# Quarter-width third blocks in the experts, a rotation on TensorE and other moved work at both ends of attention

## The chip, the cores and the metric

The kernel runs on one NeuronCore of a Trainium2 chip. Its engines work in parallel, each on its own stream of instructions in program order: PE (TensorE, matrix products, with PEld for the loads of its weights), DVE (VectorE), ACT (ScalarE), POOL (GpSimd) and SP (SyncE, which here only issues DMAs). The metric is the device time of one execution in microseconds (us). Before the change it was 4768.45 us, the median of 3 runs (4766.24 to 4772.63). A separate execution was profiled; every duration below comes from that one. Line numbers such as L761 are those of the kernel before.

## What is computed

The reference is one layer of the macaron kind: half an expert layer, attention, half an expert layer, each on a layer norm and each added to its input (8 sequences of 1024 rows, 512 wide, float32):

```
x = x + 0.5 * ffn(_layernorm(x))
x = x + attn(_layernorm(x))
x = x + 0.5 * ffn(_layernorm(x))

def ffn(x):                       # 32 experts, C = ceil(1.25 * 8192 / 32) = 320
    top1 = argmax(softmax(xt @ w_router));  gate = its probability
    pos = rank of the token among those of its expert;  accepted = pos < C
    y = (silu(buf @ w_gate) * (buf @ w_up)) @ w_down       # per expert, 320 rows
    return xt + where(accepted, y[slot] * gate, 0)

def attn(x):                      # 16 heads of 32
    q, k, v = x @ Wq.T + bq, x @ Wk.T + bk, x @ Wv.T + bv
    q, k = rope(q), rope(k)       # x * cos + rotate_half(x) * sin
    return softmax(q @ k.T / sqrt(32)) @ v @ Wo.T + bo
```

## The kernel before

**Stages.** First all rows are normalized and routed (`front`): a table in DRAM gets, for each slot of each expert, the token's number and its gate. Then the experts of the first half layer run one after the other (`experts`), then attention (`Attention.run`), whose last part also routes its result, then the experts of the second half layer. PE, DVE, ACT and POOL execute in exactly the order in which the program issues (a manual schedule); SP's DMAs are ordered by a scheduler.

**Experts.** They are sorted by their number of tokens, most first, and the code exists in four versions with fixed widths by rank (`profiles`); a switch takes the narrowest that holds all tokens. Version 0 has widths 320 (6 experts), 304 (1), 288 (5), 272 (6), 256 (3), 240 (5), 224 (3), 208 (3). An expert's rows lie in up to three blocks of 128 rows; the third holds at most 64 tokens (`last`). `feed` (L722) computes one expert: for each of four quarters f of the hidden width, `gated` (L706) makes 4 products for the gate and 4 for the up half (L712, moving size the width), ACT makes the Silu and DVE the product `a` (L736). In the same time DVE and ACT measure and normalize the rows of the following expert. Then for each block the product with `w_down` follows: 4 products of 512 columns for a full block (L753); for the third block each token takes two partitions: its 64 tokens go through two halves of the array's columns, once for the first 256 output columns and once for the last 256 (L761, 8 products of 256 columns). DVE adds the gated product to the rest of the rows (L757; L767 for the third block, 256 columns) and POOL issues the indirect DMA that puts the rows back (L771). `places` (L566) reads the table once per half layer and makes `come` (which rows to gather), `go` (where to put) and `gates`, with the third block's entries doubled for the two halves. Float32 products run as two passes, so the profile counts twice as many.

**Attention** runs over 8 sequences b and 4 groups c of four heads. `opening` (L1072) is what runs before the first products of scores: SP loads two weights and then 8 tiles of x; DVE measures a tile (`measure`), POOL takes the power -0.5, ACT normalizes, PE transposes four blocks (`turn`) and DVE (half 0) or ACT (half 1) copies the result to `hT` (`kept`, L1147). Tiles of half 0 are transposed while those of half 1 are measured. Then `project` makes k and q of half 0 (4 products each), and `rotated` (L1207) applies the rotation: DVE adds the bias and writes `raw` (L1215), 8 DMAs issued by SP exchange the halves of each head into `rot` (L1222, L1223), POOL multiplies `raw` by the cosines (L1225), DVE multiplies `rot` by the sines and adds (L1228, L1229). Only then do the scores start.

`stage` (L894) has 16 slots. A slot computes the scores `sa` (L1295) of one pair of stretches for all four heads, from which DVE takes maxima (L1310) and ACT the exponentials (L1314, `junk`), and from the second stage on also the transposed scores `sb` of the unit before, whose exponentials `pr` (L1307) are multiplied by v into `po` (L1377, `weighed`). Between, a slot has one group of products from `fill`: projections of q and k, of v (`values`), or of the output (`output`, L1387). All of these accumulate in one bank of PSUM with the tag `m`. Scores use three places `s0`, `s1`, `s2`. The first stage (b = c = 0) has no `sb` and `po`; its first 13 slots each hold a whole group.

**Attention's end.** A last stage finishes the sums of the last unit and fills slots 9 to 12 with the output of half 0 of the last sequence; in slot 14 the task `finished(b, 0)` starts, which normalizes and routes those 4 tiles: ACT normalizes (`last_rows`, L1469) and writes the kept part `rs` (`put_kept`), PE transposes, ACT copies (L214), PE computes the router's products (`routers`, L231 and L243), DVE and PE the positions (`route`), POOL scatters into the table. Behind the stage the outputs of half 1 follow, four groups, each with two steps of the task between; then `finished(b, 1)` with `sorted`, which ranks the experts for the switch. Then SP reads the table and the second experts start.

Of the kernel before, what the change touches and what calls it, by code (L numbers as in the profile page):

```python
# [22 lines left out]
P = 128  # L23
# [27 lines left out]
class Block:  # L51


    def __init__(self, nc, tc, T, D, E, F):
# [20 lines left out]
        assert all(a <= b for one, two in zip(self.profiles, self.profiles[1:])  # L75
                   for a, b in zip(one, two))

        self.copy = nc.scalar.copy
# [123 lines left out]
    def logits(self, hs, lg, pool, psum, tag, bufs=2, tags=None):  # L202

        xT = pool.tile([P, self.KD, 4 * P], F32, tag="xT", bufs=bufs, name="xT")
        j = 0
        for h in hs:
            if isinstance(h, tuple):
                yield h  # L210
                continue
            yield PE, 0.6
            if tags:
                self.nc.scalar.copy(  # L214
                    xT[:, :, j * P : (j + 1) * P], self.turned(psum, tags[j], h)
                )
            else:
                self.transposed(psum, tag, xT[:, :, j * P : (j + 1) * P], h)
            j += 1
        yield from self.routers(xT, lg, pool, psum, tag, bufs=1)  # L220
# [289 lines left out]
    def experts(self, table, ranks, src, dst, weights, loaded=None, others=None):  # L510
# [16 lines left out]
        for i in tc.Switch(which, len(self.profiles)):  # L527
            widths = self.profiles[i]
            with (
# [12 lines left out]
                following = expert.gather(1, widths[1])  # L542
                for r in range(E):
                    if following:
                        following.weights = self.load(
                            wp, order, r + 1, weights, hold=None if r else "wg"
                        )
# [6 lines left out]
class Expert:  # L554
# [7 lines left out]
    def places(self, table, matrix):  # L562
# [9 lines left out]
        )  # L572
        rows = ap.tile([R, P, 2], F32, tag="slots", bufs=1, name="slots")
        nc.sync.dma_start(rows, table[0 : s.NS, :].rearrange("(r s) c -> r s c", s=P))
# [8 lines left out]
        for i in range(2):  # L583
            p = slice(i * n, (i + 1) * n)
            nc.vector.tensor_scalar(
                self.go[p, R - E : R], ids[p, R - E : R], 2.0, float(i), ALU.mult, ALU.add
            )

    def begin(self, to):
# [87 lines left out]
    def rests(self, to):  # L677

        s, n, half = self.s, self.s.last, self.s.D // 2
        for i in range(min(to.NB, s.NB - 1)):  # L680
            s.rest(to.x[:, i, :], to.x[:, i, :], to.by, i)
        if to.NB == s.NB:
            to.rest = self.ap.tile([P, half], F32, tag="rest", name="rest")
            for i in range(2):
                p = slice(i * n, (i + 1) * n)
                s.rest(
                    to.rest[p, :], to.x[p, s.NB - 1, i * half : (i + 1) * half], to.by,
                    s.NB - 1, p,
                )
# [30 lines left out]
    def feed(self, now, following, after):  # L720
# [3 lines left out]
        nc, s = self.nc, self.s  # L724
        n, half, KF = s.last, s.D // 2, s.KF
        a, wd = s.acts[now.r % 2], now.weights[2]
# [14 lines left out]
        for i in range(now.NB):  # L741
# [16 lines left out]
            else:  # L758
                for f in range(KF):
                    for c in range(2):  # L760
                        nc.tensor.matmul(  # L761
                            yp[c * n : (c + 1) * n, 0:half], a[:, f, i * P : s.C],
                            wd[:, f, c * half : (c + 1) * half],
                            start=(f == 0), stop=(f == KF - 1),
                        )
                ys = ys[:, 0:half]
                nc.vector.scalar_tensor_tensor(  # L767
                    ys, yp[:, 0:half], gate, now.rest, ALU.mult, ALU.add
                )
                to = to.rearrange("t (c d) -> (t c) d", c=2)  # L770
            nc.gpsimd.indirect_dma_start(  # L771
# [6 lines left out]
class Attention:  # L778
# [13 lines left out]
    def __init__(  # L792
# [14 lines left out]
        self.tasks, self.behind, self.half, self.now = [], [], None, 0  # L807
        self.credit, self.biased = 0.0, False
        self.hT, self.w_qk, self.qk, self.v, self.oT = ({} for _ in range(5))
# [113 lines left out]
    def run(self):  # L923
        nc, tc = self.nc, self.tc
        F, KD = mybir.EngineType, self.KD
        with (
# [6 lines left out]
            with tc.manual_schedule(engines={F.PE, F.Activation, F.DVE, F.Pool}):  # L933
                self.s.copy = nc.vector.tensor_copy
                later = self.opening()
                units = [(b, c) for b in range(self.B) for c in range(KD)]
                for i, (b, c) in enumerate(units):
                    self.stage(
                        (b, c), units[i - 1] if i else None, self.fill(b, c, later),
# [4 lines left out]
                    None, units[-1], dict(zip((9, 10, 11, 12), self.output(b, 0))),  # L944
                    {14: [(2, self.finished(b, 0))]}, whole=True,
                )
                self.last_sums()
                for f in self.output(b, 1):
                    at_once(f())
                    self.now += 1  # L950
                    for _ in range(2):
                        self.step(100)
                        self.product()
                self.start(self.finished(b, 1, self.ranked))
# [54 lines left out]
    def constants(self, wp):  # L1009
# [5 lines left out]
        for i, a in enumerate((bq, bk, bv)):  # L1015
# [4 lines left out]
            self.bias[:, 0, :], self.bias[:, 0, :], self.scale, None, ALU.mult  # L1020
        )
        self.ident16 = wp.tile([P, P], BF16, name="ident16")
        nc.vector.tensor_copy(self.ident16, s.ident)
# [76 lines left out]
    def opening(self):  # L1100
# [40 lines left out]

        def turn(half, j):
            x = xs[half][j]
            s.normalize(x, x, bys[half][1], j)
            return s.turned(psum, f"s{j % 3}", x)

        def kept(half, j, tp):  # L1147
            copy = nc.scalar.copy if half else nc.vector.tensor_copy
            copy(self.hT[0, half][:, :, j * P : (j + 1) * P], tp)  # L1149

        for j in range(4):
            measure(0, j)
        for j in range(4):
            measure(1, j)
            kept(0, j, turn(0, j))
        at_once(steps[-1])
        self.there |= {(0, 0), (0, 1)}
        q0, k0, k1, q1 = self.project(0, 0)
        for f in (k0, q0):
            at_once(f())  # L1160
        for j in range(4):
            kept(1, j, turn(1, j))
            self.now += 1
            self.step(100)
        self.load(2)
        while self.tasks:
            self.now += 1
            self.step(100)
        return [k1, q1]
# [9 lines left out]

    def project(self, b, c):  # L1180

# [7 lines left out]
        for which, n in ((0, 0), (1, 0), (1, 1), (0, 1)):  # L1189

            def group(n=n, which=which):
                assert (b, n) in self.there, (b, c, n)
                if n == 0:
                    name = "qk"[which]
                    dst[which] = pool.tile([P, self.L], F32, tag=name, bufs=3, name=name)
                acc = self.psum.tile([P, 512], F32, tag="m", name="pq")
                for k in range(KD):
# [5 lines left out]
                    )  # L1203
                self.start(self.rotated(dst[which], b, c, which, n, acc), rank=0)

            work.append(group)
        return work  # L1207

    def rotated(self, dst, b, c, which, n, acc):
# [22 lines left out]
    def values(self, b):  # L1232
# [3 lines left out]
        for t in range(LT):  # L1236

            def group(t=t):
                v = self.pool.tile([P, D], F32, tag="v", bufs=12, name="v")
                acc = self.psum.tile([P, D], F32, tag="m", name="pv")  # L1240
                hT, at = self.hT[b, t // 4], t % 4 * P
# [188 lines left out]
    def finished(self, b, half, counted=None):  # L1430
# [39 lines left out]
        def last_rows():  # L1470
            while self.weighted < half:
                yield WAIT, 1
            for j, x in enumerate(self.kept[half]):
                h = pool.tile([P, D], F32, tag="h3", bufs=3, name="h3")
                s.normalize(h, x, by, j)
                if not half:
                    put_kept(j)
                yield h

# [129 lines left out]
```

## Time and profile before

| stage of the profiled execution | us from the start | length | PE busy | DVE busy | ACT busy | granted PE clock |
|---|---|---|---|---|---|---|
| normalizing and routing | 0 to 176 | 176.0 | 102.6 | 129.9 | 92.4 | 0.74 |
| first experts | 176 to 930 | 754.0 | 753.9 | 275.5 | 153.1 | 1.00 |
| attention's opening | 930 to 972.3 | 42.3 | 16.7 | 18.2 | 9.8 | 0.67 |
| its first stage | 972.3 to 1051 | 78.7 | 70.1 | 58.3 | 48.3 | 0.96 |
| stages between and sums of the last | 1051 to 3911 | 2860.0 | 2803.0 | 2025.8 | 2510.8 | 1.00 |
| last outputs, routing, first gather | 3911 to 3990 | 79.0 | 37.4 | 26.6 | 19.4 | 0.65 |
| second experts | 3990 to 4756 | 766.0 | 755.2 | 276.7 | 108.8 | 0.99 |

The profiled execution took 4757.85 us, of which its span, from the first to the last record, is 4756.0 us. The table is a view by windows: for each stretch the time in which each engine was busy, and the mean clock that PE was granted as a share of full speed. A busy PE need not be at its peak, since products overlap in the array.

### The profile page before, as it was taken

To read this page: it belongs to the slowest core of one execution; us is meant where nothing else is said; L and a number is where in the kernel's file an instruction comes from. 1 tells how busy PE (TensorE), PEld (TensorE's weight loads), DVE (VectorE), ACT (ScalarE), POOL (GpSimd) and SP (SyncE) were. 2 spreads that over 40 slices of the span, in tenths; PEclk is the share of its full clock that TensorE was granted. 3 is DMA by queue.
4 is the path that set the end of the run, shared out by engine and by line. 5 is a ranking of instruction groups with operands and counts; after the bars stand their busy time and mean duration, and the time that the engine had idled before them with its cause. 6 is when DMAs were issued, how large, how long until landed. Compare 5 with 4: busy or idle time off the path is not lost.

```text
span 4756.0 us, 68742 instructions
## 1 busy us (share of the span) xinstructions
PE 4538.9 (95%) x24532; PEld 2114.6 (44%) x24532; DVE 2811.0 (59%) x5542; ACT 2942.7 (62%) x5890; POOL 788.9 (17%) x798
## 2 busy tenths in 40 slices
PE   6799999888999999999999999999999986999999
PEld 4466677632233333333333333333333324666777
DVE  8433333367667777767767767777777743333332
ACT  6211212159998888888888888888888861111111
POOL 4433333210000000100010110110110002222221
PEclk7899999989999999999999999999999997999999
DMA  4556666511112212212212212212212114555564
GB/s 144 164 178 205 196 201 231 198 30 37 35 30 61 75 39 65 72 39 68 71 39 67 70 43 65 72 39 70 67 41 58 52 41 150 168 173 175 177 207 141
DMA packets 288503, 482.09 MB, mean 101 GB/s; under 512 B 47608, under 2 KB 82882, under 8 KB 288146
## 3 DMA queue, kind: packets, MB, share of 16 engines
q1 hardware_dynamic: 253554, 400.95, 26.9%
q0 software_dynamic: 34304, 76.41, 5.2%
q8 instruction: 196, 3.21, 0.3%
q14 instruction: 161, 1.32, 0.1%
q10 hardware_dynamic: 288, 0.20, 0.0%
HBM read 376.18 MB, written 89.46 MB: 98 GB/s over the span
## 4 chain that ended last, share of the span: by engine, by line
PE 82%; DVE 7%; ACT 4%; issue 3%; DMA 2%; POOL 1%; SPq 1%; DVEq 0%; POOLq 0%; ACTq 0%
PE sa L1295 13%; PE gp L712 9%; PE up L712 9%; PE pq L1200 9%; PE po L1377 9%; PE yp L753 9%; PE sb L1275 6%; PE px L1411 4%; PE pv L1245 4%; PE sb L1302 3%; ACT junk L1314 2%; DVE nm L1310 2%; PE yp L761 1%; PE tp L700 1%; PE tp L196 1%
## 5 line engine op out<-in xcount | busy, mean ns | idle before, releaser
L1310 DVE TENSOR_REDUCE nm<-sa 128x2 f32<-128x1024 f32 x1024 | 1249.0, 1221 | 652.0 <-PE sa L1295 392.3
L1314 ACT ACTIVATE junk<-sa,nm 128x512 f32<-128x512 f32 x2048 | 1407.3, 687 | 271.9 <-DVE nm L1310 191.7
L1295 PE MATMUL sa<-k,q 32*128 32x512 f32 x4096 | 1144.6, 643 | 13.0 <-ACT pr L1307 4.2
L1307 ACT ACTIVATE pr<-sb 128x1024 f32<-128x1024 f32 x1024 | 1040.7, 1018 | 107.8 <-PE sb L1302 104.4
L1302 PE MATMUL sb<-q,k 32*128 32x512 f32 x4096 | 1063.4, 603 | 0.0
L717 ACT ACTIVATE sg<-gp 128x320 f32<-128x320 f32 (+7 forms) x256 | 99.6, 389 | 1122.1 <-PE gp L712 1120.9
L1225 POOL TENSOR_TENSOR raw<-raw,a 128x512 f32<-128x512 f32 x128 | 164.5, 1285 | 2388.7 <-DMA rot<-raw 1571.3
L1377 PE MATMUL po<-pr,v 128*32 128x512 f32 x4096 | 549.4, 608 | 0.1
L1200 PE MATMUL pq<-hT,wqk 128*128 128x512 f32 x1024 | 507.6, 619 | 8.0 <-DVE hT L1149 4.4
L712 PE MATMUL gp<-bT,wg 128*128 128x272 f32 (+7 forms) x2048 | 509.2, 392 | 0.0
L712 PE MATMUL up<-bT,wu 128*128 128x272 f32 (+7 forms) x2048 | 503.5, 389 | 0.0
L753 PE MATMUL yp<-wd,a 128*128 128x512 f32 x1024 | 460.3, 592 | 0.0
L1275 PE MATMUL sb<-mrow,ones 3*128 3x512 bf16 x2048 | 393.0, 385 | 43.7 <-ACT pr L1307 41.2
L712 PEld LDWEIGHTS gp<-bT,wg 128*128 128x128 f32 x2048 | 384.7, 191 | 98.4 <-issue 26.7
L712 PEld LDWEIGHTS up<-bT,wu 128*128 128x128 f32 x2048 | 386.6, 190 | 75.4
L1275 PEld LDWEIGHTS <-ones 3*128 3x128 bf16 x2048 | 99.6, 91 | 712.8 <-issue 673.2
L736 DVE TENSOR_TENSOR a<-sg,up 128x320 f32<-128x320 f32 (+7 forms) x256 | 110.7, 433 | 506.5 <-PE up L712 368.9
L1314 ACT ACTIVATION_READ_ACCUMULATOR junk<-sa,nm 128x1 f32 x2048 | 398.1, 194 | 0.0
L1302 PEld LDWEIGHTS sb<-q,k 32*128 32x128 f32 x4096 | 360.3, 184 | 0.1
L1295 PEld LDWEIGHTS sa<-k,q 32*128 32x128 f32 x4096 | 303.2, 183 | 70.7 <-ACT pr L1307 30.4
L1200 PEld LDWEIGHTS pq<-hT,wqk 128*128 128x128 f32 x1024 | 175.0, 190 | 324.5 <-issue 225.3
L757 DVE SCALAR_TENSOR_TENSOR ys<-yp,gates,x 128x512 f32<-128x512 f32 x128 | 96.1, 751 | 337.2 <-PE yp L753 337.2
(183 smaller groups left out, 4231.5 us busy)
## 6 DMA issues: line engine op xcount, KB each, us to landing
wg<-in_w_gate SPq DMA_DIRECT2D x64, 1024.0 KB
wu<-in_w_up SPq DMA_DIRECT2D x64, 1024.0 KB
wd<-in_w_down SPq DMA_DIRECT2D x64, 1024.0 KB
rot<-raw SPq DMA_DIRECT2D x1024, 32.0 KB
all<-in_x SPq DMA_DIRECT2D x32, 512.0 KB
xt<-first_rows SPq DMA_DIRECT2D x64, 256.0 KB
xr<-first_rows SPq DMA_DIRECT2D x64, 256.0 KB
d<-inverse SPq DMA_DIRECT2D x256, 64.0 KB
```

What stands on the lines that cost most here:

```text
L712: nc.tensor.matmul(acc, w[:, k, f * P : (f + 1) * P], to.bT[:, k, 0:width], start=(k == 0), stop=(k == s.KD - 1),)
L753: nc.tensor.matmul(yp, a[:, f, i * P : (i + 1) * P], wd[:, f, :], start=(f == 0), stop=(f == KF - 1),)
L1200: nc.tensor.matmul(acc, w[:, which, k, :], self.hT[b, n][:, k, :], start=(k == 0), stop=(k == KD - 1),)
L1245: nc.tensor.matmul(acc, hT[:, k, at : at + P], self.w_vo[:, k, :], start=(k == 0), stop=(k == KD - 1),)
L1275: nc.tensor.matmul(sb[:, h, :], self.ones16[at : at + 3, :], row[at : at + 3, :], start=True, stop=False,)
L1295: nc.tensor.matmul(sa[:, h, :], qa[at, (g * 4 + j) * P : (g * 4 + j + 1) * P], ka[at, m * 512 : (m + 1) * 512], start=True, stop=True,)
L1302: nc.tensor.matmul(sb[:, h, :], k[at, t * P : (t + 1) * P], q[at, n * 512 : (n + 1) * 512], start=False, stop=True,)
L1307: nc.scalar.activation(pr, sb, AF.Exp)
L1310: nc.vector.tensor_reduce(nm[:, m, j, pair : pair + 2], sa, AX.X, ALU.max, negate=True)
L1314: nc.scalar.activation(self.junk, sa[:, h - pair, :], AF.Exp, bias=nm[:, m, j, h : h + 1], accum_out=se[:, m, j, h : h + 1],)
L1377: nc.tensor.matmul(self.po[at : at + HD, :], self.v[b][t][:, c * P + at : c * P + at + HD], prs[h // 2 * 2][:, h % 2, :], start=(t == 0), ...
L1411: nc.tensor.matmul(acc, self.oT[b, c, half][:, j * P : (j + 1) * P], self.w_vo[:, c, :], start=False, stop=(c == KD - 1),)
```

## The change

1. **Third blocks of at most 32 tokens by quarters.** For widths over 256 and up to 288 a token takes four partitions, each with 128 output columns: 16 products of 32 weight columns and 128 moving columns in place of 8 of 64 and 256. `rest`, the DVE sum and the scattered rows follow. A new function makes the table entries for these experts, once per half layer, before expert 2 is fed.
2. **Opening.** Half 0 is measured, transposed and copied (ACT and DVE in turn) ahead of the measuring of half 1; k and q of half 0 are projected into two banks; their bias is added on ACT, and the exchange of halves is a product with a permutation (`turn`, built by 8 small POOL copies) instead of 8 DMAs each.
3. **First stage.** Its groups accumulate in the banks `m` and `po` in turn.
4. **Ends.** `finished(b, 0)` starts in slot 13 instead of 14; one step instead of two between the last output groups; copies of the router's transposes alternate between ACT and DVE; the last four rows are all normalized first, two on ACT and two on DVE.

```diff
+    def parts(self, width):
+        s = self.s
+        return 1 if width <= (s.NB - 1) * P else 4 if width <= s.quarter else 2
+    def quarters(self, widths):
+        few = [r for r, width in enumerate(widths) if self.parts(width) == 4]
...
+        nc.vector.tensor_copy(
+            rows[last, :, :],
+            self.rows[last, 0:n, :].rearrange("r s c -> r (s c)").unsqueeze(1)
+            .to_broadcast([E, 4, n * 2]),
+        )
+        for i in range(2):
+            pt = self.ps.tile([P, len(few)], F32, tag="tp", name="pt")
+            nc.tensor.matmul(
+                pt, rows[last, :, i], self.matrix[last, at], start=True, stop=True
+            )
+            if i == 0:
+                nc.vector.tensor_scalar(self.come[:, at], pt, float(s.T - 1), None, ALU.min)
+                for k in range(4):
...
+                    nc.vector.tensor_scalar(
+                        self.go[p, at], pt[p, :], 4.0, float(k), ALU.mult, ALU.add
+                    )
+            else:
+                nc.vector.tensor_copy(self.gates[:, at], pt)
@@ experts
                 for r in range(E):
+                    if r == 2:
+                        expert.quarters(widths)
@@ feed
-                    for c in range(2):
+                    for c in range(parts):
                         nc.tensor.matmul(
-                            yp[c * n : (c + 1) * n, 0:half], a[:, f, i * P : s.C],
-                            wd[:, f, c * half : (c + 1) * half],
+                            yp[c * n : (c + 1) * n, 0:part], a[:, f, i * P : i * P + n],
+                            wd[:, f, c * part : (c + 1) * part],
@@ run
-                    {14: [(2, self.finished(b, 0))]}, whole=True,
+                    {13: [(2, self.finished(b, 0))]}, whole=True,
...
-                    for _ in range(2):
-                        self.step(100)
-                        self.product()
+                    self.step(100)
+                    self.product()
@@ opening
         for j in range(4):
             measure(0, j)
+            if j:
+                normalize(0, j - 1)
+        at_once(steps[-1])
+        for j in range(4):
+            if j == 3:
+                normalize(0, j)
+            turn(0, j)
+        q0, k0, k1, q1 = self.project(0, 0, True)
         for j in range(4):
             measure(1, j)
-            kept(0, j, turn(0, j))
         at_once(steps[-1])
+        at_once(k0())
         for j in range(4):
-            kept(1, j, turn(1, j))
+            normalize(1, j)
+        at_once(q0())
+        self.now += 1
+        self.step(100)
+        for j in range(4):
+            turn(1, j)
@@ project, values
-                acc = self.psum.tile([P, 512], F32, tag="m", name="pq")
+                acc = self.psum.tile([P, 512], F32, tag=self.bank(), name="pq")
+    def bank(self):
+        if not self.early:
+            return "m"
+        self.turns += 1
+        return ("m", "po")[self.turns % 2]
+    def turned(self, dst, b, c, which, n, acc):
+        raw = pool.tile([P, 512], F32, tag="raw", name="raw")
+        nc.scalar.activation(
+            raw, acc, AF.Identity, bias=self.bias[:, which, c : c + 1],
+            scale=self.scale if which == 0 else 1.0,
+        )
+        yield WAIT, 1
+        rot = self.psum.tile([P, 512], F32, tag=f"s{which}", name="rot")
+        nc.tensor.matmul(rot, self.turn, raw, start=True, stop=True)
+        away = pool.tile([P, 512], F32, tag="rot", name="rot")
+        nc.vector.tensor_tensor(away, rot, self.sn[:, cols], ALU.mult)
+        nc.gpsimd.tensor_tensor(raw, raw, self.cs[:, cols], ALU.mult)
+        nc.vector.tensor_tensor(dst[:, cols], raw, away, ALU.add)
@@ logits
-                self.nc.scalar.copy(
+                (self.nc.vector.tensor_copy if j % 2 else self.nc.scalar.copy)(
@@ last_rows
-                h = pool.tile([P, D], F32, tag="h3", bufs=3, name="h3")
-                s.normalize(h, x, by, j)
+                tag, bufs = ("xt", 4) if half else ("h3", 3)
+                h = pool.tile([P, D], F32, tag=tag, bufs=bufs, name="h3")
+                (s.normalize_ if half and j % 2 else s.normalize)(h, x, by, j)
+                hs.append(h)
                 if not half:
                     put_kept(j)
-                yield h
+                    yield h
+            if half:
+                yield from hs
```

## The prediction

> **What bounds the kernel now.** I read the page first: the busy tenths and the shares of the chain that ended last.
>
> ```profile
> PE   6799999888999999999999999999999986999999
> ...
> PE 82%; DVE 7%; ACT 4%; issue 3%; DMA 2%; POOL 1%; SPq 1%; DVEq 0%; POOLq 0%; ACTq 0%
> ```
>
> PE carries the chain except in three places: the start, attention's opening (slice 8) and its end (slice 33). So an edit counts if it shortens PE's stream in the experts, or a chain of other engines in those gaps. Next the timeline of PE in an expert of width 288 (start, length, engine, line, operation, tiles, passes).
>
> ```profile
> 388.13 3.60 PE L753 MATMUL yp<-wd,a 128*128 128x512 f32 x8
> 391.66 1.95 PE L761 MATMUL yp<-wd,a 128*64 128x256 f32 x16
> 393.54 2.21 PE L712 MATMUL gp<-bT,wg 128*128 128x288 f32 x8
> ```
>
> Eight passes of 512 columns take 3.44 us on the path, 0.43 each, so the full block ends its streaming at 391.57, and the next expert's gp starts at 393.54: the third block costs 1.97. Two column halves run side by side: 8 rounds of 256 columns at 0.216 are 1.73, and 0.24 goes into changing the array's tiling and back. No wait stands between: PE alone sets this stretch.
>
> The chain of waits in the opening (start, length, what):
>
> ```profile
> 951.95 5.23 PE pq L1200 x8
> 957.20 0.76 DVE raw L1215
> 957.98 0.63 SPq L1222
> ...
> 967.49 1.94 DMA rot<-raw
> 969.68 1.80 POOL raw L1225
> 972.34 2.09 PE sa L1295 x8
> ```
>
> Sixteen DMA issues of about 0.63 us stand in line on SP, and q's rotation waits for the last. In the first stage, the timelines of DVE and PE (brackets: idle time before it, and its releaser):
>
> ```profile
> 993.80 0.69 DVE L1229 TENSOR_TENSOR q<-raw,rot 128x512 f32<-128x512 f32 x1 [1.16 <-POOL raw L1225]
> 994.60 0.75 DVE L1215 TENSOR_SCALAR raw<-pq,bias 128x512 f32<-128x512 f32 x1
> ...
> 995.40 3.70 PE L1200 MATMUL pq<-hT,wqk 128*128 128x512 f32 x8 [1.13 <-DVE raw L1215]
> ```
>
> PE waits for the single bank, but DVE is late because it stood still for POOL. The chain at the end of attention:
>
> ```profile
> 3914.89 0.70 DVE xr L1415
> ...
> 3916.60 0.82 ACT h L174
> ...
> 3921.24 5.18 PE px L1411 x8
> ...
> 3937.34 0.70 DVE xr L1415
> ```
>
> Four output groups of 3.75 us (15.0) are spread over 26.2 us (3911.1 to 3937.3): PE waits for the first tile's normalizing, loses its clock (5.18 for 3.43), and waits again.
>
> **The change, part by part.**
>
> *Quarters.* The groups by form show gp products of width 288 in 320 passes and of 272 in 384; an expert has 32, so 10 and 12 experts, 22 in all, change. That also shows that version 0 ran in both half layers. A new block has 32 passes of 128 columns; four column groups side by side make 8 rounds of 0.108 (a quarter of 0.43), 0.86, plus the same 0.24: 1.10, a gain of 0.87, 22 x 0.87 = 19.1. Whether 32-column groups run side by side is shown by the sums of v, PEld being the loads:
>
> ```profile
> 1504.43 0.16 PEld L1377 LDWEIGHTS po<-pr,v 128*32 128x32 f32 x8 [0.76 <-issue]
> 1504.44 1.06 PE L1377 MATMUL po<-pr,v 128*32 128x512 f32 x8
> ```
>
> Eight passes take 0.99 in the chain, not 3.44, and eight loads fit in 0.16. Whether passes can follow so fast (0.027 apart on average) no row shows over 32 passes. The fastest train of full-width passes is this:
>
> ```profile
> 1030.50 0.38 PE L1350 MATMUL tp<-ident,pieces 128*128 128x128 bf16 x4 [0.78 <-DVE v L1249]
> 1030.72 0.27 PE L1353 MATMUL tp<-ident,sum 128*16 128x128 f32 x1
> ```
>
> Four passes in 0.22, 0.055 each. Bounds per block: a gain of 0.87 (rounds full) and none (0.054 apart, the rate of this row). I take 0.87, since loads and passes of po, nearest in shape, come within 0.02 of each other.
>
> [...]
>
> The new table entries make PE wait before expert 2: after expert 1's third block DVE makes `ys` (0.48), copies 32x256 (0.4, between L575's 0.22 for 128 columns and L703's 0.42 for 256), then PE makes two small products (four passes of L578 took 1.14 at half clock; 0.5 here): 1.5 against 0.1 now, twice, +3.0 (bounds 2 and 5). Queued behind this wait is all of expert 2, so it is paid in full. DVE's six table writes (some 0.25 each, L580) put the measuring of expert 3 back by about 2.5; its normalized rows are ready 9 us before their transposes (400.2 against 409.2), `a` of the first quarter 5 us before its bank is wanted (398.1, 403.3). `rest` in four pieces costs at most twice two of 0.41; DVE is busy 275 of 754 us there. Without that cover it would be 22 x 0.8 = 18. The scatter keeps its 0.98 on POOL and its 128 rows, half as long.
>
> *Opening.* Followed in the rows' durations from the third normalizing's end, 945.1: ACT copies two tiles (0.58 each; the second waits for transposes until 946.3) and then normalizes the fourth (0.81): 947.7; transposes 1.1, DVE's copy 0.7: k starts at 949.7 instead of 951.95. k 5.2 (half clock first) to 954.9; q follows at once in its own bank, to 958.4. On ACT k's bias takes 0.8, then the four normalizings of half 1 stand ahead of q's bias: 959.8. The exchange products take 0.86 each; DVE's sines 0.7, POOL's cosines 1.3 to 1.8, DVE's sum 0.7: k done at 962.0, q at 963.8. The transposes of half 1 wait for the place `s0`, read by DVE until 962.7, and take 16 x 0.11: the scores start at 964.6 instead of 972.3. I take 7.5; 5 if these transposes run at half clock (0.27 each), 9 if k's products run at full clock. The eight POOL copies of `turn` (0.55 each, as POOL's smallest, L165) run from the last scatter's landing, 933.8, to 938.3, ahead of the first power at 940.9; gone that cover, each us late is one lost. SP loses 16 issues and nothing is put in their place.
>
> *Two banks.* PE's waits for `m` in the first stage sum to 4.5 us. But between 984 and 1016 DVE has no free time: maxima 2.36, rotation 1.9 to 2.5 with POOL's wait inside, bias 0.75, more than PE's 4.7 per slot. With the second bank PE meets the occupied score places next. Stepping slot by slot through 16 slots with these durations (PE 1.07 + 3.63, DVE as said, ACT 0.81 per exponential) gives 1050.4 with one bank (1050.9 in the trace) and 1049.1 with two: a gain of 1.3; bounds 0 and 3.
>
> *End.* One tile is now normalized in slot 15, behind the last `pr` on ACT; its transposes stand ahead of the last four sums on PE, which delays the outputs by 1.3 (ACT 0.81, PE 0.45). After that every group finds its tile: 1.3 + 15.0 + 3 x 0.45 = 17.7, to 3928.8 instead of 3937.3. On SP the first `rs` store now stands ahead of the four loads of x for these groups, so they leave at 3912 instead of 3902; eight loads needed 4.3 us in the opening (935.18), so the first lands at about 3916.3 with its product done at 3916.1. Then measuring 1.65, the router's copy and products, and half 0's maxima and sums on DVE (3.2) ahead of half 1's scale: 3935.9 instead of 3943.6. Four tiles in pairs on ACT and DVE take 6.3 to the last copy (now 10.2), but DVE has half 0's positions (2.7) ahead of half 1's router copy: 3944.9 instead of 3955.78. What follows is the same, so 10.9; I take 10.5. Bounds: 6 (loads and transposes late, half clock) and 13 (full clock to the end).
>
> The sum: -19.1 + 3.0 - 7.5 - 1.3 - 10.5 = -35.4. The profiled execution (span 4756.0, 1.85 around it, 4757.85) would take 4722.4; it stands 10.6 below the median of the runs. On the median: 4768.45 - 35.4 = 4733.0.
>
> **The rivals.**
> - *The quarters gain nothing*, the 0.054 bound. For it: no row shows such a train of passes. Against: the loads in 0.16. Then +3.0 - 19.3 = -16.3: 4752.
> - *The ends give back.* Chains in gaps run at half clock (0.67 and 0.65 in these stages), and loads moved behind stores can be late: 5 + 0 + 6 instead of 19.3, so -27.1: 4741. Against: after the change PE has fewer gaps there. With the first rival too: -8, 4760.
> - *Slower: the four column groups don't overlap.* Place: L761 of 22 experts. At 0.108 per pass a block costs 32 x 0.108 + 0.24 = 3.70, 1.73 more, +38; with +3.0 and -19.3 the time is 4790. The whole breaks even at 0.077 per pass; slower by over 9.5 us from 0.091. Against: po at 0.99 for eight passes.
> - *It doesn't do what it says*: other widths or another version would leave the blocks alone. The routing of the first half is untouched and the 22 experts are counted, so I give this no chance.
>
> **How the numbers follow.** Forecast 0.70; quarters for nothing 0.10; ends give back 0.12; both 0.03; slower 0.05. Within 0.2% (9.5 us, about what a measurement of this kernel can tell from no change) lie the case of both and 0.03 of the first two: same 0.06, slower 0.05, faster 0.89. The likeliest: 4733. The bounds of its parts add to -42.1 at best (19.1 - 2 + 9 + 3 + 13), 4726, and the runs of before lie 6.4 apart: 4720 below. Upward the first two rivals are taken in, 4752, and the 4.2 from the median to the slowest run: 4757 with the next microsecond.
>
> **What would show it.** In the experts: L761 in 32 passes, gp 1.1 us after the full block's end, periods of 272-wide experts at 24.06 instead of 24.93; a wait for DVE of about 1.1 before expert 2. In the opening: first sa about 42.3 - 7.5 after the last expert's end. In the first stage: no PE wait for `raw`, new ones for ACT. At the end: no output group at 5.2, and half 1's router copy some 34 us after the last sum (now 44.8). I am wrong if the block stays near 1.97, or if the stages between the ends change their length (2860).

## The result and the profile after

The changed kernel takes 4730.6 us (median of 4 runs, 4725.5 to 4735.1) beside 4769.6 for the kernel before (4 runs, 4766.2 to 4772.6): a ratio of 0.992, 95% interval 0.990 to 0.994, some 39 us less. 4733 was forecast. In a second set it took 4730.3 beside 4768.2 (0.9925, 0.991 to 0.994).

The page of the changed kernel: the busy tenths of TensorE and the shares of the chain that ended last.

```profile
PE   6699999898999999999999999999999986999999
...
PE 83%; DVE 7%; ACT 4%; issue 3%; DMA 2%; POOL 1%; SPq 0%; DVEq 0%; POOLq 0%; ACTq 0%
```

The shape is the same; SPq, to which the 16 issues in a line at the opening belonged (some 10 us of the chain), has gone from 1% to 0%. Where the time went is seen only stage by stage. The stages below are cut at TensorE's own starts, in the profiled execution of each kernel (4757.85 and 4731.47):

| stage | before | after | difference | forecast |
|---|---|---|---|---|
| start to the first gp | 175.7 | 186.7 | +11.0 | 0 |
| experts 1, to the last expert's first gp | 735.9 | 728.7 | -7.2 | -8.1 |
| opening, from there to the first sa | 60.7 | 55.7 | -5.1 | -7.5 |
| first stage, to the first po | 91.3 | 88.1 | -3.3 | -1.3 |
| the rest, to the last mrow product | 2843.1 | 2842.5 | -0.6 | 0 |
| end, to the next first gp | 83.4 | 70.0 | -13.4 | -10.5 |
| experts 2, to the last product | 754.4 | 746.6 | -7.8 | -8.1 |

Without the start the change is worth 37.3 here, and 35.4 was forecast. The start has another story (before_again below).

TensorE and DVE at the end of an expert of width 288 (start, length, engine, line, operation, tiles, passes; brackets: idle before it and its releaser):

```profile
401.48 3.60 PE L797 MATMUL yp<-wd,a 128*128 128x512 f32 x8
...
405.01 1.08 PE L805 MATMUL yp<-wd,a 128*32 128x128 f32 x32
...
406.02 1.24 PE L755 MATMUL gp<-bT,wg 128*128 128x288 f32 x4
```

The full block has streamed its eight passes by 401.48 + 3.44 = 404.92, and gp starts at 406.02: 1.10 for the third block, as forecast, where the half-columns took 1.97. All 22 experts went from 25.78 to 24.91 (width 288) or from 24.92 to 24.06 (272); the last of width 272 from 24.49 to 23.62. The others kept their periods to 0.02, experts 0 and 1 aside (expert 0's first products run at half clock in both kernels, for 1.1 before, from 175.7 to 176.8, and for 2.6 after, from 186.7 to 189.3: 28.00 before and 28.77 after).

The wait that the tables cost, ahead of expert 2:

```profile
243.06 0.48 DVE L811 SCALAR_TENSOR_TENSOR ys<-yp,gates,rest 128x256 f32<-128x256 f32 x1 [1.14 <-PE yp L805]
243.58 0.28 DVE L610 COPY four<-slots 32x256 f32<-32x256 f32 x1
...
244.01 0.61 PE L618 MATMUL pt<-matrix,four 32*128 32x11 f32 x4 [0.99 <-DVE four L610]
...
244.54 2.42 PE L755 MATMUL gp<-bT,wg 128*128 128x320 f32 x8
```

TensorE stands 0.99 behind DVE's copy, which itself stands behind `ys`, and then runs two products of 0.53 together. The period of expert 1 is 29.08 in place of 27.48: 1.60, twice 3.2.

The opening, TensorE and what it waits for:

```profile
954.30 8.62 PE L1258 MATMUL pq<-hT,wqk 128*128 128x512 f32 x16 [0.78 <-DVE hT L1199]
...
962.75 2.07 PE L1286 MATMUL rot<-raw,turn 128*128 128x512 f32 x4
...
963.86 2.49 POOL L1289 TENSOR_TENSOR raw<-raw,a 128x512 f32<-128x512 f32 x2 [4.46 <-PE rot L1286]
965.16 1.73 DVE L1290 TENSOR_TENSOR k<-raw,rot 128x512 f32<-128x512 f32 x1 [0.65 <-POOL raw L1289]
966.82 0.68 DVE L1288 TENSOR_TENSOR rot<-rot,a 128x512 f32<-128x512 f32 x1
967.55 3.62 PE L199 MATMUL tp<-ident,xt 128*128 128x128 f32 x16 [2.73 <-DVE rot L1288]
971.10 1.14 PE L1379 MATMUL sa<-k,q 32*128 32x512 f32 x8
```

No DMA is left in this chain. Three things are to be seen. The two products take 8.62: the granted clock is half until 957.3, so the first 3.0 of k's passes run at half clock. DVE's sum of k takes 1.73, where the sum of q, with POOL idle, takes 0.69: POOL multiplies in the same time. And half 1's transposes wait 2.73 for a place that the second exchange holds, and then run at 0.22 each: the granted clock is half from 967.6 to 971.0.

The end, from the last output group:

```profile
3919.63 3.60 PE L1495 MATMUL px<-wvo,oT 128*128 128x512 f32 x8
3923.27 0.69 DVE L1499 TENSOR_TENSOR xr<-xr,px 128x512 f32<-128x512 f32 x1 [1.88 <-PE px L1495]
...
3929.80 0.15 DVE L170 SCALAR_TENSOR_TENSOR nmr<-mv,rstd 128x4 f32<-128x4 f32 x1
...
3932.62 2.03 PE L199 MATMUL tp<-ident,h 128*128 128x128 f32 x12
...
3937.42 0.68 DVE L241 COPY parts<-pl 128x512 f32<-128x512 f32 x1
```

No output group takes 5.2 any more. Half 1's scale comes 28.2 after the last mrow product (which starts at 3901.63; 36.5 before), and `parts` 7.6 after the scale (12.4 before).

### The profile page after: what moved, and what is told of

Read it like the earlier page. It is cut to its first block, busy times and chain, and to the rows that moved or that the text cites. A ratio compares the mean times of both kernels' runs of the same rounds, so it can differ in the third digit from the quotient of the medians.

```text
span 4729.7 us, 69515 instructions
## 1 busy us (share of the span) xinstructions
PE 4519.9 (96%) x24896; PEld 2111.9 (45%) x24896; DVE 2827.4 (60%) x5604; ACT 2939.7 (62%) x5886; POOL 789.1 (17%) x806
## 4 chain that ended last, share of the span: by engine, by line
PE 83%; DVE 7%; ACT 4%; issue 3%; DMA 2%; POOL 1%; SPq 0%; DVEq 0%; POOLq 0%; ACTq 0%
PE sa L1379 14%; PE gp L755 10%; PE pq L1258 9%; PE up L755 9%; PE po L1461 9%; PE yp L797 9%; PE sb L1359 6%; PE px L1495 4%; PE pv L1329 4%; PE sb L1386 3%; ACT junk L1398 2%; DVE nm L1394 2%; PE tp L199 2%; PE tp L743 1%; ACT pr L1391 1%
```

## The experiments

Twelve runs, in four sets; each set stands beside the kernel before on the same chip. Four of them are single runs: row_order, one_bank, places and scale_first; before_again is a fifth, of the kernel before. They are read mainly by their profiles.

**q_only and no_q: are the parts additive?** The kernel before with the quarters alone, and the changed kernel without them:

```diff
+                    if r == 2:
+                        expert.quarters(widths)
...
-                    for c in range(2):
+                    for c in range(parts):
...
```

That is q_only's edit to the kernel before (with `parts`, `quarters`, `rests` and the scatter as in the change); no_q has every other hunk of the change and none of these.

> The kernel before with the third blocks by quarters alone (the tables' entries with them); opening, first stage and end stay as before. Theory (the four column groups run side by side, each of the 22 blocks gains 0.87, the tables cost 1.6 twice): -19.1 + 3.2 = -15.9 on 4769.6, so 4754; widths 288 and 272 at periods of 24.91 and 24.06, expert 1 at 29.08; opening 60.7, first stage 78.6, end 83.3 as in the profile of before. Rival (the experts' weights or gathers become late when the experts are shorter by 22 us, and the gain is given back in the wider experts or in the next stage): periods of 25.8 and 24.9 again or other widths longer by 0.5 and more, 4765 to 4772.

> The changed kernel without the quarters: opening, two banks and end as changed, third blocks by halves as before. Theory (the parts add up, as the stages of the two profiles have it: opening -5.1, first stage -3.3, end -13.3, middle -0.8): -22.5 on 4769.6, so 4747. Rival (the ends' gain of the profile is partly the shorter experts', which free SP and the transfers earlier): less than 18 gained, 4752 and more.

q_only: 4738.8 beside 4756.0, ratio 0.9963 (0.9951 to 0.9976): -17.2. no_q: 4731.7, ratio 0.9948 (0.993 to 0.997): -24.3. Together -41.5, and the whole had -39: they add up within the intervals. In q_only's profile experts 1 take 729.0 and experts 2 746.2, as in the changed kernel, opening 62.2 (60.7 and 62.7 in the two profiles of the kernel before) and end 81.8 (83.4 in both); in no_q the end takes 68.9. So neither rival holds: the experts' gain isn't given back, and the ends don't live on it.

**row_order: do the column groups run side by side?**

```diff
-                for f in range(KF):
-                    for c in range(parts):
+                for c in range(parts):
+                    for f in range(KF):
```

> The changed kernel with the 32 passes of a third block in another order: all eight passes of one column group, then of the next. Theory (a pass of 128 columns takes 0.108 and only passes of different groups that stand next to each other overlap): 32 x 0.108 + 0.24 = 3.70 for a block in place of 1.10, periods of 27.5 and 26.7, 22 x 2.60 = 57 more, about 4788. Rival (what counts is the number of passes and columns; passes of 32 columns follow at some 0.027 in any order): 1.10 for a block, 4731.

4758.6 in one run, some 38 to 41 over what the changed kernel's two ratios (0.9925 and 0.9918) give beside a kernel before of 4756. The timeline of the same block:

```profile
422.30 3.60 PE L797 MATMUL yp<-wd,a 128*128 128x512 f32 x8
425.83 2.46 PE L805 MATMUL yp<-wd,a 128*32 128x128 f32 x32
428.22 1.97 PE L755 MATMUL gp<-bT,wg 128*128 128x288 f32 x7
```

428.22 - 425.74 = 2.48 for the block, neither 1.10 nor 3.70. (The edit turns the 14 blocks in halves round as well: their periods go from 27.48 to 28.40. 22 x 1.38 + 14 x 0.92 = 43.) The single records in the trace show how. They don't name the group; they are sorted here into four rows by their spacing of 0.109:

```
starts of passes of L805 in us; four column groups, one after the other
group 1: 425.830 425.963 426.072 426.181 426.291 426.400 426.509 426.618
group 2: 426.296 426.430 426.539 426.648 426.757 426.866 426.976 427.085
group 3: 426.763 426.896 427.006 427.115 427.224 427.333 427.442 427.551
group 4: 427.230 427.363 427.472 427.581 427.691 427.800 427.909 428.018
```

Within a group a pass follows the last by 0.109, the 0.108 of the sum. The next group begins 0.466 later, right behind the start of the fifth of the eight passes of the group ahead, with three still to start: two groups run side by side, not four. So passes of different groups do overlap, and the order that takes the groups in turn is what fills the array. Why the next group doesn't begin earlier, no run shows.

**one_bank: what is the second bank worth?**

```diff
-                    self.early = i == 0
+                    self.early = False
```

> The changed kernel with one bank in the first stage; the opening keeps its two. Theory of the prediction (DVE sets the stage's pace, the second bank is worth 1.3): from the first sa to the next stage's first products 75.6 becomes 76.9, with PE waits for raw of some 2. Rival (the second bank is worth all 3.3 that the stage lost): 78.9, PE waits for raw and v of 4 to 5 as before. Second rival (the stage is shorter because the opening leaves PE at full clock and DVE less in arrears): 75.6, no change.

one_bank: 4717.4 in one run beside 4756.0, 38.6 less and so no worse than the changed kernel's 39: the whole is too coarse for this question, and so are the marks of the expectation. To the next stage's first products it takes 76.3, between the expected 75.6 and 76.9, but the changed kernel has 74.2 and 75.2 there (two profiles). To the first po it takes 89.6, where kernels with two banks have 87.2 to 89.6 (ten profiles) and those before 90.6 to 92.0. Both marks take in the first scores, at a clock that differs, and the stage's end, from the 14th group of sa to the first po, which takes 21.9 to 23.6 with either number of banks. Between the starts of the second and the fourteenth group of sa lie twelve slots: 61.5, 61.8, 62.0 and 62.1 in the four profiles with one bank (before_again, before, q_only, one_bank), 60.0 to 61.2 in the ten with two, mean 60.5. The ranges don't meet, and one_bank, with the changed opening, stands with the old kernels: nothing in these slots is seen to come from the opening. The waits of TensorE in that stage of one_bank (engine and line, what it waited for, us, times, longest):

```profile
PE sa L1379 <- ACT junk L1398: 3.4, 3, 2.0
PE pq L1258 <- DVE raw L1299: 2.5, 3, 0.9
...
PE pv L1329 <- DVE v L1333: 1.0, 2, 0.7
```

With two banks (the changed kernel) the waits for raw and v are gone, those for ACT stay (2.9 before, 3.5 after). The bank is worth 1.3 between the means (0.3 to 2.1 between single profiles), as forecast; between the first two profiles it was 1.5. Most of the stage's other 1.8 lies at its beginning. In the timeline of before its first products were

```profile
972.34 2.09 PE L1295 MATMUL sa<-k,q 32*128 32x512 f32 x8 [3.14 <-DVE q L1229]
974.36 4.25 PE L1200 MATMUL pq<-hT,wqk 128*128 128x512 f32 x8
```

at half clock after a wait of 3.14; in the profile of the changed kernel the first sa takes 1.14 and the products 3.70, as the clock came back 0.1 ahead of them: 0.95 + 0.55 = 1.5. That share is partly chance: in after_again the half clock reaches 2.4 into the stage and the first sa takes 2.09 again. The first slot is 6.2 to 6.8 long in the three profiles with the old opening, 4.7 to 5.8 in the others.

**after_again and before_again: the longer start.**

> The changed kernel once more, beside the others on this chip. Theory (its profile's start, 186.7 to the first gp where every other profile has 175.5 to 176.4, was a chance of that one execution): first gp at 176, and the whole 38 to 41 under the kernel before. Rival (the change itself makes the start longer): first gp at 186 to 187 again.

> The kernel before, profiled once more. Theory (the start up to the first gp, 175 to 176 in some profiles and 182 to 187 in others of the same code, goes with the chip or its job and not with the kernel): on a chip where the kernel before takes some 4768 its profile has the first gp at 182 to 187, on one where it takes some 4756 at 175 to 177; the stages behind it as in its first profile, opening 60.7, end 83.4. Rival (the kernel before always starts at 175.7, the longer start belongs to kernels with the changed opening): 175 to 177 in both cases.

after_again: 4730.3, first gp at 185.9. That theory fell: it was no chance of one execution. before_again: 4756.9, first gp at 175.3, beside a kernel before of 4759.0, which both allow. Over all profiles: in the sets where the kernel before takes 4756 and 4759 the first gp comes at 175.3 to 176.4, in seven profiles, six of them with part or all of the change; in those where it takes 4768 to 4770 at 182.2 to 187.2, for the changed kernel, after_again, places, scale_first, best and warm14. So the start goes with the set: the same code (best) had 187.2 in one and 175.6 in another, and six profiles with part or all of the change start as early as the kernel before. The profile of before that the prediction used had the short start, though its other runs had 4768: that fits the 10.6 by which it stood under the median. What delays the start wasn't found (of two sets on a chip with the number 15 one is of either kind), and no profile of the kernel before with the long one was taken.

**places, scale_first, best: what the change left.** The three waits seen in the profile after, each taken away by order and places alone. places:

```diff
-            tp = s.turned(psum, ("s0", "s1", "s2", "m")[j], xs[half][j])
+            tags = (("s0", "s1", "s2", "m"), ("s2", "po", "s1", "m"))[half]
+            tp = s.turned(psum, tags[j], xs[half][j])
+        nc.gpsimd.tensor_tensor(dst[:, cols], raw, self.cs[:, cols], ALU.mult)
         yield WAIT, 1
         rot = self.psum.tile([P, 512], F32, tag=f"s{which}", name="rot")
...
-        nc.gpsimd.tensor_tensor(raw, raw, self.cs[:, cols], ALU.mult)
-        nc.vector.tensor_tensor(dst[:, cols], raw, away, ALU.add)
+        nc.vector.tensor_tensor(dst[:, cols], dst[:, cols], away, ALU.add)
```

scale_first, with one step in place of two between half 1's power and its scale:

```diff
-                self.start(self.finished(b, 1, self.ranked))
+                self.start(self.finished(b, 1, self.ranked), rank=0)
...
-            while self.weighted < half:
-                yield WAIT, 1
```

best has both, and DVE's copy to `four` one expert earlier:

```diff
+                    if r == 1:
+                        expert.fours()
                     if r == 2:
                         expert.quarters(widths)
```

> The changed kernel with another use of places in the opening: the transposes of half 1 begin in s2 and po, which are free, and take s1 and m last (s0, s1, s2, m in the changed kernel), and the cosine's product goes straight to its place in k and q on POOL, so that it needn't wait for the exchange on TensorE. Theory (PE stands 2.7 waiting for s0 behind the second exchange, and DVE's sum of k takes 1.73 in place of 0.69 while POOL multiplies): the transposes begin about 2.6 earlier against k's first product, opening 52.4 to 53.2 in place of 55. Rival (q is done no earlier, or DVE and POOL hinder each other as before, so that the scores wait for q): 54.5 to 55.5.

> The changed kernel with half 1's scale at the end of attention set right behind its power on POOL and half 1's four normalizings with it, ahead of half 0's maxima and positions on DVE. Theory (the scale waits 3.1 behind half 0's route on DVE, and the four normalizings with it): from the last mrow product to the next half layer's first gp 66 to 67 in place of 69 to 70. Rival (half 0's maxima and positions, 5.9 of DVE, stand ahead of half 1's maxima in any order): within 0.7 of 69 to 70.

> The changed kernel with the places and the cosine of the opening, half 1's scale first at the end, and the tables' wider copy on DVE one expert earlier, so that PE finds it done. Theory (the wait at expert 2 is for the copy behind ys alone): expert 1 at 27.9 in place of 29.08 in both half layers, with the other two 2.4 + 2.3 + 2.8 = 7.5 under the changed kernel. Rival (the wait is for the place that the products take, or what is saved in front of the experts is lost at the first of them): expert 1 stays at 29, 0 to 4 under the changed kernel.

places: opening 50.4, 5.3 under after_again where 2.6 were expected, but 1.4 of it lies ahead of the first pq, which the edit doesn't touch. The timeline:

```profile
960.17 2.07 PE L1288 MATMUL rot<-raw,turn 128*128 128x512 f32 x4
...
962.03 0.94 DVE L1291 TENSOR_TENSOR k<-k,rot 128x512 f32<-128x512 f32 x1
962.07 1.91 PE L199 MATMUL tp<-ident,xt 128*128 128x128 f32 x16
...
964.51 1.14 PE L1380 MATMUL sa<-k,q 32*128 32x512 f32 x8 [0.52 <-DVE q L1291]
```

From the first pq to the first sa 13.0 in place of 16.9 (after_again). Of these 3.9, 2.9 lies between exchange and transposes, which now follow without a gap; the other 1.1 lies in the products (8.83 in place of 9.92), which had half clock for 3.4 in place of 5.6 and which the edit doesn't touch. The transposes keep the clock: 1.91, where the changed kernel's first profile had 3.62 at half clock and after_again 2.46, with the half clock reaching into the first scores (2.09 for 1.14). That the wait cost the clock is seen over all profiles: in the six with the changed opening and its wait (after, after_again, no_q, row_order, one_bank, scale_first) the granted clock falls to half for 3.4 close to the first scores, in the five with free places (places, best, best_again, warm, warm14) it does not. In the whole the single run of places had 4723.7, 6.6 under the median of the changed kernel, but its profile is only 1.4 shorter than after_again's.

scale_first: the end takes 68.4, beside 69.0 (after_again): the rival was right. (Its single run had 4721.7; its profile is 3.2 shorter than after_again's, which the shorter start, 182.2 for 185.9, makes up alone.) The scale did come 2.9 earlier, and then:

```profile
3920.53 3.68 PE L199 MATMUL tp<-ident,h 128*128 128x128 f32 x16 [1.30 <-ACT h L177]
...
3925.08 1.93 PE L234 MATMUL pl<-xT,w_router 128*32 128x512 f32 x8 [0.87 <-DVE xT L217]
3927.07 0.69 DVE L241 COPY parts<-pl 128x512 f32<-128x512 f32 x1 [2.14 <-PE pl L234]
3927.82 0.80 PE L306 MATMUL pp<-oh,before 128*128 128x128 f32 x2 [0.80 <-DVE parts L241]
```

at half clock (1.93 where the changed kernel has 1.06), with half 0's products and positions now between half 1's `parts` and its next product. `parts` is 3.0 earlier than in after_again, that next product 1.4, the first gp 0.65. In after_again the clock was full again from 32.2 to 39.0 after the last mrow product; here it stays at half from 25.5 on.

best: 4721.3 (4719.7 to 4723.4) beside 4730.3 (4724.9 to 4733.0) for the changed kernel in the same set, 9.0 less, ratio to before 0.9904 (0.989 to 0.992). Expert 1's period is 28.05, 1.03 less, twice:

```profile
240.68 1.95 PE L813 MATMUL yp<-wd,a 128*64 128x256 f32 x16
242.56 0.63 PE L626 MATMUL pt<-matrix,four 32*128 32x11 f32 x4
243.12 2.42 PE L763 MATMUL gp<-bT,wg 128*128 128x320 f32 x8
```

There is no wait left, only the two products. Opening 51.7 (-4.0), end 68.7 (-0.3) and 2.1 make 6.4 of the 9; the rest is within what single profiles differ by elsewhere (from the first po to the last mrow product it is 2838 to 2843 in any kernel).

**best_again, warm, warm14: the clock of the opening.** The edit to best in warm; warm14 has 14 in place of 30:

```diff
+        idle = psum.tile([P, 4, P], F32, tag="po", name="idle")
+        for _ in range(30):
+            nc.tensor.matmul(
+                idle, s.ident, s.ident.unsqueeze(1).to_broadcast([P, 4, P]),
+                start=True, stop=True,
+            )
         xs = [fetch(0)]
```

> The version with free places, half 1's scale and the tables' copy first, once more, as the measure for the next one. 8 to 9 under the changed kernel as in its first run: a ratio to the kernel before of 0.990 to 0.991.

> The same version with 30 products of no use (the identity by itself, 512 columns each, into the free place po) ahead of the opening's first transposes, in the 13 us in which PE waits for x. Theory (the granted clock falls to half some 3 after the experts' end and rises again only some 3.4 after PE is busy, so the last transposes and k's product run at half clock: 1.1 for 0.55 and 5.2 for 3.5): from the first pq to the first sa 11.2 in place of 12.9, the opening 49 to 50 in place of 51.7, and the whole 2 to 2.5 under the version without them. Rival (the products are late themselves, or x's gaps between the transposes lose the clock again): k's product at 5.2 as before, opening 51.5 or longer.

> As warm, with 14 products of no use: each took 0.866 in the run before (two passes of 0.43; the expectation there took one pass), so that 30 ran 26.0 and held up the first transposes by some 13. Theory (14 x 0.866 = 12.1 end before x is normalized, 13.7 after the experts' end, and the clock stays full as in the run before): from the first pq to the first sa 11.3 in place of 12.9, opening 49.5 to 50.2 in place of 51.7 to 52.3, the whole some 2 under the version without them: a ratio to the kernel before of 0.9898 beside 0.9902 to 0.9904, which lies inside the intervals; the profile decides. Rival (without work up to the first transposes the clock is lost in the gaps): first pq to first sa 12.9 again.

best_again: 4711.5 beside 4759.0, 0.9902 (0.989 to 0.992), as before. warm: 4715.7, 0.9915, 4.2 slower. I had counted one pass of 0.43 for a product that has two; 30 products took 26.0 and held up the transposes (opening 60.7). But behind them everything ran at full clock:

```profile
948.04 1.47 PE L199 MATMUL tp<-ident,xt 128*128 128x128 f32 x12
950.90 0.66 PE L199 MATMUL tp<-ident,xt 128*128 128x128 f32 x4 [1.39 <-ACT xt L177]
952.34 7.13 PE L1273 MATMUL pq<-hT,wqk 128*128 128x512 f32 x16 [0.78 <-DVE hT L1214]
```

11.3 from the first pq to the first sa (12.9 and 13.4 in best's two profiles), as the theory had it. With 14 the products end in time, at 944.4, and the clock is lost in the gaps behind them, at 948.1:

```profile
946.88 0.66 PE L199 MATMUL tp<-ident,xt 128*128 128x128 f32 x4 [0.60 <-ACT xt L177]
948.92 1.12 PE L199 MATMUL tp<-ident,xt 128*128 128x128 f32 x4 [1.39 <-ACT xt L177]
950.82 9.18 PE L1273 MATMUL pq<-hT,wqk 128*128 128x512 f32 x16 [0.78 <-DVE hT L1214]
```

13.4 from the first pq to the first sa: the rival. 4721.1 beside 4769.1, 0.9898 (0.988 to 0.992), the same as best within the intervals. That such products between the transposes would hold the clock was not tried.

## Why the prediction was right, step by step

- *Quarters, 22 x 0.87.* Right to the hundredth: 22 blocks, 1.10 for each. That passes of four groups run side by side was read from eight loads in 0.16 and from po; the starts of the passes and row_order show that it is so, and that it hangs on the order in which the passes are issued. The first rival (no gain, 0.054 a pass) and the one on the slower side (no overlap) are refuted: less the 0.24 of the sum, 1.10 is 0.027 a pass. In the block above 0.09 stands ahead of the first pass (405.01), 0.02 more in the first round than in the others and 0.11 behind the last: 0.22. Behind a full block with no third one the next product starts after its 3.44 (911.98 to 915.42). That the change of the array's tiling takes this time is the author's estimate; no run took it apart.
- *Tables, +3.0.* 3.2 measured; the mechanism as forecast, a copy behind `ys`, and best takes two thirds of it away.
- *Opening, -7.5.* -5.1 in the two profiles, the lower bound; between three profiles with the old opening (60.7, 62.2, 62.7) and six with the new one (54.3 to 55.8, mean 55.4) some 6.5. The mechanism was right, the term mis-sized is the transposes of half 1: priced at 0.11 each, they ran at 0.22 after a wait of 2.7, which cost 1.8. The forecast had them wait for `s0` too, but kept the half clock for its lower bound. DVE's sum of k at 1.73 for 0.7 lay inside that wait. The first landing of x was another 0.9 late in that profile.
- *Two banks, -1.3.* The bank itself 1.3 to 1.5, as stepped through, but the stage lost 3.3: that its first products would run at full clock, or at half clock for a shorter time, was in no term. It was worth 1.5 in this pair of profiles.
- *End, -10.5.* -13.4, just beyond the bound of 13 for full clock. To the scale 8.3 in place of 7.7. From scale to `parts` 4.8 in place of 3.2: the forecast had 9.0 behind the scale, of which 6.3 to the last copy and 2.7 for half 0's positions; measured 5.6 and 2.0. The positions ran in part while TensorE made half 1's router products, and TensorE, at half clock until 3933.7, was at full clock for these (1.06). The delay of the last sums, forecast at 1.3, was 1.3 (4.99 from the last mrow product to the last po, 3.69 before). The rival in which the ends give back is refuted by no_q.
- *The sum.* -35.4 forecast, -37.3 in the profiles behind the start, -39.0 and -37.9 by the medians. The experts (15.0 for 16.1, most of it expert 0's clock) and the opening gave 1.1 and 2.4 less, the first stage and the end 2.0 and 2.9 more. So the mechanisms held, but that the sum comes within 2 to 4 is in part luck: misses of 3.5 on one side and 4.9 on the other cancel. That the sum made against the profile could be carried to the median needed the long start to fall on both kernels alike; the ratios in sets of either kind (0.9902 and 0.9904 for best) say that it does.

## What to carry to other kernels

Column groups filled the array only when passes of different groups followed each other closely (1.10 for a block, 2.48 in the other order): take the groups in the inner loop, and see whether a block too narrow to fill them can be cut further; here twice the passes lost nothing to their count. Look at what runs behind a wait of TensorE, and at which clock: here the granted clock fell to half at the end of a wait of 2.7, and the transposes behind it took 3.62 in place of 1.91. When a stage is rebuilt, look at the places and in-place products that its parts share: the opening's wait went by naming a free bank and writing a product straight to its destination (the two were not tried apart), the tables' by making one copy an expert earlier.

## What the runs showed of the hardware

- With the groups in turn, a round's four passes start 0.007 apart and the next round 0.109 later (405.249, .256, .262, .269, then 405.358); with the groups one after the other the next group's passes start 0.466 behind the last group's, when three of its eight are still to start.
- In the profiles of the kernel before and of the changed kernel the granted clock has two values, full and half, and each stretch of either but the last lasts 3.41 or a whole multiple of it (3.41, 10.24 and 20.48 in the opening of the changed kernel). It fell 2.2 to 5.2 after the experts' last product in the twelve profiles in which TensorE then stood idle (4.7 in the kernel before, at 934.55; 3.1 in the changed kernel, at 936.84). Single profiles of one kernel differ by where these steps fall (the first sa takes 1.14 in the changed kernel's first profile, 2.09 in after_again). The clock came back 3.0 and 3.4 after TensorE began work without a gap in the opening of the changed kernel (954.30 to 957.32, 967.55 to 970.97), 3.1 and 3.2 in the kernel before (951.95 to 955.03, 972.34 to 975.51), and 4.9 at the end of its attention (3919.70 to 3924.63).
- The granted clock held through gaps of 1.39 and 0.78 after 26 of unbroken work (warm), and was lost with bursts of 0.66 between gaps of 0.48 to 1.39 (warm14, TensorE busy for 1.97 of the 3.6 up to the fall).
- DVE's addition of 512 columns took 1.73 beside a multiplication on POOL and 0.69 by itself.
- The start of the program differs by 6 to 12 between sets of runs (175.3 to 176.4 and 182.2 to 187.2 to the first gp), also for the same kernel.
